# A two-layer graph network on one core: the order of the block pieces, the degree's copy and the split rows' buffers

## The chip, the core and the metric

The kernel runs on one core of a Trainium2 chip. The metric is the device time of one launch in microseconds (us); lower is better. A core has five engines that work side by side: TensorE (PE in the profile) for matmuls, VectorE (DVE) and ScalarE (ACT) for elementwise work, GpSimd (POOL), which here only issues the gathers, and SyncE (SP), which issues most of the other transfers. Each engine takes its instructions in one order that is fixed when the kernel is built, and waits at an instruction until what it depends on is there.

## The reference

There are 12,500 nodes with 256 features, and 200,000 edges sorted by their target. Both layers take the mean over each node's incoming edges:

```python
def _sage_conv(x, src, dst, W_l, b_l, W_r):
    msgs = x[src]
    agg = segment_sum(msgs, dst, num_segments=N_NODES)
    deg = segment_sum(ones, dst, num_segments=N_NODES)
    mean = agg / maximum(deg, 1.0)[:, None]
    return mean @ W_l + b_l + x @ W_r

h = relu(_sage_conv(x, src, dst, W1_l, b1, W1_r))
h = relu(_sage_conv(h, src, dst, W2_l, b2, W2_r))
out = layernorm(x + h @ W3 + b3)
```

Targets with low numbers have many edges, those with high numbers few: a target is about 12,500 times the square of a uniform number.

## The kernel before

**Two ways to sum.** Nodes lie in 98 blocks of 128. For the first targets (5 groups of 256 in layer 1, 7 in layer 2) the kernel counts the edges between every source and target into a table and multiplies it with the source rows: `count` (L622) builds the table, `product` (L604) multiplies it with rows that were split into three bf16 parts, and `degrees` (L698) sums it. `split_rows` (L598) makes the parts of x, one block at a time, with `exact` (L590): ScalarE casts, VectorE subtracts, ScalarE casts, VectorE subtracts. All this is called dense work. The other edges are gathered: `gathered` (L526) takes 4 x 128 edges in a round, fetches their source rows with four indirect transfers (L532) and sums edges with the same target by matmuls (L543). `summed` (L552) adds the result into a ring of eight blocks, `sums` and `degs`, at a place that is read from the data.

**A block's pieces.** When all edges of a block are summed, the block is finished in pieces, written as a generator. `first_block` (L852) has three in layer 1. The first loads 128 rows of x. The second turns the block's degree row into a column by a tiny matmul (L860); VectorE takes the maximum with 1 (L862) and the reciprocal (L863), and `transposed` (L812) turns the x rows with two matmuls by the identity (L814) and a ScalarE copy (L816). The third runs `sage` (L833), two matmuls by each weight, VectorE's L842 and L843, and the relu (L845), clears the ring's place, and stores h and its three parts. `last_block` (L876) has five: load h and x rows; turn the h rows; `sage`; turn the result; multiply by W3 and normalise. Blocks of the dense groups run through the same code without the degree and the clearing.

**What sets the order.** `layer` (L483) writes out the order of the TensorE and GpSimd instructions by hand. In each of its rounds (269 in layer 1, 247 in layer 2) it issues the gathers and their matmuls, then some pieces of blocks, half of the dense work that is due, the sum of the round before, more pieces, and the other half. At most `MOST` = 3 blocks are in work. A round advances a quarter of all pieces that are left, rounded up, half of them before the sum and half after; a call takes the blocks in turn from the oldest, one piece each. `begin` starts a waiting block by its first piece. Dense work is metered by costs, so that it ends eight rounds before the last. The orders of VectorE, ScalarE and SyncE come from a scheduler.

**Buffers.** Rows of x have three buffers named `x_sb`, which the split rows and the blocks share (L804). `rest` in `exact` has one buffer, which they share too, `parts` has two, and the PSUM tile `block_ps` two.

Of the kernel before, what the change touches and what calls it, by code (L numbers as in the profile page):

```python
# [7 lines left out]
F32 = mybir.dt.float32  # L8
# [5 lines left out]
OP = mybir.AluOpType  # L14
# [7 lines left out]
P = 128  # L22
# [25 lines left out]
def by_runs(  # L48
# [429 lines left out]

    AHEAD = 2

    MOST = 3

    def layer(table, hot, block, n_pieces, dense, dense_cost):  # L483


        queue, waiting, done = [], [], set()

        def advance(i):
            b, p, left = queue[i]
            next(p)  # L490
            queue[i] = b, p, left - 1
            if left == 1:
                done.add(b)
                del queue[i]
                return True

        def begin():
            while waiting and len(queue) < MOST:
                b, *of = waiting.pop(0)
                queue.append((b, block(b, *of), n_pieces))  # L500
                advance(len(queue) - 1)

        def pieces(n):

            i = 0
            for _ in range(min(n, len(queue))):
                if not advance(i):
                    i += 1
            begin()

        filler = dense(waiting)
# [58 lines left out]
        for i in range(len(rounds) + 1):  # L570

            last, before = gathered(i) if i < len(rounds) else None, last
            n = -(-sum(left for _, _, left in queue) // 4)
            pieces(-(-n // 2))
            due = dense_cost * min(1.0, (i + 1) / (len(rounds) - 8))
            fill(spent + (due - spent) * 0.5)
            if before:
                summed(*before)
                while begun < left_after(before[0]):
                    waiting.append((begun,))  # L580
                    begun += 1
                begin()
            pieces(n // 2)
            fill(due)
        fill(1e8)
        while queue or waiting:
            pieces(MOST)


    def exact(t, s):  # L590

        rest = work.tile([P, D], F32, name="rest", bufs=1)
        nc.scalar.copy(s[:, 0], t)
        nc.vector.tensor_tensor(rest, t, s[:, 0], op=OP.subtract)
# [217 lines left out]
    def transposed(t, ps, name):  # L812
        for c in range(NC):
            nc.tensor.transpose(ps[:, c], t[:, c * P:(c + 1) * P], ident)  # L814
        s = work.tile([P, NC, P], F32, name=name)
        nc.scalar.copy(s, ps[:, :NC])  # L816
        return s

    def ring(b):

# [12 lines left out]
    def sage(own_t, b, agg, wl, wr, bias, name):  # L833

        ps = block_pool.tile([P, 2, D], F32, name="block_ps")
        for c in range(NC):
            nc.tensor.matmul(ps[:, 0], lhsT=agg[:, c], rhs=wl[:, c], start=c == 0, stop=c == NC - 1)  # L837
# [7 lines left out]
        nc.scalar.activation(h, own, AF.Relu)  # L845
        return h

    def turned():
        t = block_pool.tile([P, 2, D], F32, name="block_ps")
# [2 lines left out]
    def first_block(b, agg=None):  # L852
        x_sb = load_rows(x, N, b, "x_sb")
        of_ring = agg is None
        yield True
        ps = turned()
        if of_ring:
            overlap(b, True)
            agg, deg_row = ring(b)
            nc.tensor.matmul(ps[:, NC, 0:1], lhsT=deg_row, rhs=ones[0:1, 0:1], start=True, stop=True)  # L860
            deg = work.tile([P, 1], F32, name="deg")
            nc.vector.tensor_scalar(deg, ps[:, NC, 0:1], 1.0, None, op0=OP.max)  # L862
# [12 lines left out]

    def last_block(b, agg=None):  # L876
        h_sb = load_rows(h_d, NB * P, b, "h_sb")
        x_sb = load_rows(x, N, b, "x_sb")
        of_ring = agg is None
        yield True  # L880
        if of_ring:
            overlap(b, False)
            agg, _ = ring(b)
        h_t = transposed(h_sb, turned(), "own_t")
        yield True
        h2 = sage(h_t, b, agg, w2l_sb, w2r_sb, biases[:, 1], "h")
        if of_ring:
            nc.scalar.copy(agg, zeros)
        nc.vector.tensor_add(x_sb, x_sb, biases[:, 2])
        yield True  # L890
        h2_t = transposed(h2, turned(), "own_t")
        yield True
        y = block_pool.tile([P, 2, D], F32, name="block_ps")
        for c in range(NC):
            nc.tensor.matmul(y[:, 0], lhsT=h2_t[:, c], rhs=w3_sb[:, c], start=c == 0, stop=c == NC - 1)  # L895
# [12 lines left out]
        nc.sync.dma_start(out[b * P:b * P + n, :], z[:n])  # L908
        yield True
# [383 lines left out]
```

## Time and profile before

| | |
|---|---|
| median of 3 runs | 2927.65 us (2920.19 to 2936.41) |
| the profiled execution's own time | 3466.66 us |
| its span, first to last instruction | 3464.9 us |
| mean granted TensorE clock | 0.868 |
| gathers (L532), layer 1 | 1076 x 1007 ns, from 27.2 to 1850 us |
| gathers (L532), layer 2 | 988 x 956 ns, from 1888.6 to 3405 us |
| dense product (L614) | 7056 matmuls, 289 ns |
| count casts (L688) | 1052 x 681 ns |
| turning x, h and the result (L814) | 196 x 348, 196 x 305 and 196 x 314 ns |
| own_t copy (L816) | 294 x 374 ns |
| HBM traffic | 582.80 MB read, 89.87 MB written |

The profile is of one execution, which took longer than the median of the runs without a profiler. In the views an operand pair `out<-in` tells what an instruction writes and reads, `x2` how many records a row merges (an fp32 matmul leaves two), and `[1.07 <-PE block_ps L860]` that its engine stood idle for 1.07 us until that instruction released it. A wait's three numbers are the sum in us, how often, and the longest.

### The profile page before, as it was taken

What the parts mean: (1) busy time and instruction counts of PE and PEld (TensorE: products, weight loads), DVE (VectorE), ACT (ScalarE), POOL (GpSimd) and SP (SyncE); (2) the same over time, 40 slices, a digit from 0 to 9 for tenths busy, and PEclk for the clock granted to TensorE, in tenths of its full rate; (3) what the DMA queues carried; (4) which work ended last, traced back from release to release, by engine and by line L of the source; (5) the groups of instructions that cost most, each with busy time, mean ns of one, the idle gap of its engine ahead of it and who ended that gap; (6) DMA issues with size and microseconds to landing.
All of it is one profiled execution on the core that took longest, in us unless ns stands there. A gap on an engine that the chain in (4) does not pass through costs nothing.

```text
span 3464.9 us, 54167 instructions
## 1 busy us (share of the span) xinstructions
PE 2583.9 (75%) x18630; PEld 1705.5 (49%) x18630; DVE 1468.1 (42%) x4350; ACT 1250.0 (36%) x2702; POOL 2029.7 (59%) x2074
## 2 busy tenths in 40 slices
PE   2544658778878878888886677777878887878885
PEld 1121225545545556656654354444555555656664
DVE  7656655444444444445453023333223233333433
ACT  1323655455554555556553013333111111111222
POOL 3554656665665565666663666666666666566661
PEclk9666679879979989989998888888889899999998
DMA  4544577648648648656753565666777787766762
GB/s 89 153 147 147 183 210 229 195 128 279 202 144 269 202 144 263 207 159 194 222 162 111 184 204 184 187 186 192 243 240 246 243 258 240 230 211 215 223 213 69
DMA packets 408134, 676.45 MB, mean 195 GB/s; under 512 B 59659, under 2 KB 266537, under 8 KB 407849
## 3 DMA queue, kind: packets, MB, share of 16 engines
q1 hardware_dynamic: 303415, 400.51, 36.8%
q0 software_dynamic: 99072, 270.66, 25.8%
q10 hardware_dynamic: 5362, 1.72, 0.3%
q8 instruction: 149, 2.44, 0.3%
q14 instruction: 136, 1.11, 0.1%
HBM read 582.80 MB, written 89.87 MB: 194 GB/s over the span
## 4 chain that ended last, share of the span: by engine, by line
PE 60%; issue 8%; another core or an unknown queue 8%; DVE 4%; DMA 3%; ACT 3%; SPq 0%; POOL 0%; ACTq 0%; DVEq 0%
PE dense_ps L614 22%; PE part_ps L543 8%; PE block_ps L837 6%; PE count_ps L682 6%; PE block_ps L839 5%; PE sum_ps L555 4%; PE block_ps L814 3%; PE block_ps L895 3%; ACT counts L688 1%; PE sum_ps L560 1%; DMA rows<-x_d 1%; DMA rows<-h_d 1%; PE count_ps L686 1%; DVE pick L637 1%
## 5 line engine op out<-in xcount | busy, mean ns | idle before, releaser
L532 POOL DMA_INDIRECT got<-in_x_dram,src_t x1076 | 1083.2, 1007 | 764.9 <-PE part_ps L543 282.7
L532 POOL DMA_INDIRECT got<-h_d,src_t x988 | 944.4, 956 | 610.1 <-issue 247.9
L614 PE MATMUL dense_ps<-counts,rows 128*128 128x256 bf16 x7056 | 1025.9, 289 | 84.3 <-issue 49.3
L688 ACT CAST counts<-count_ps 128x392 f32 (+2 forms) x1052 | 716.1, 681 | 633.2 <-PE count_ps L686 145.9
L614 PEld LDWEIGHTS <-rows 128*128 128x128 bf16 x7056 | 702.3, 103 | 338.0 <-issue 142.4
L543 PE MATMUL part_ps<-got,one 128*32 128x257 f32 (+1 forms) x4128 | 384.9, 438 | 96.2 <-issue 47.1
L682 PE MATMUL count_ps<-pick,low 128*128 128x392 bf16 (+2 forms) x1052 | 371.1, 381 | 104.8 <-DVE pick L637 33.3
L637 DVE TENSOR_SCALAR pick<-steps,key_t 128x686 bf16<-128x686 f16 (+2 forms) x748 | 300.0, 411 | 254.1 <-PE count_ps L682 77.3
L466 DVE TENSOR_TENSOR one<-lo_t,lane_b 128x128 f32<-128x128 bf16 x516 | 148.0, 287 | 539.6 <-PE part_ps L543 143.6
L549 ACT COPY some<-part_ps 128x257 f32<-128x257 f32 (+1 forms) x361 | 136.8, 379 | 562.0 <-remote 215.5
L567 DVE TENSOR_TENSOR sums<-sums,sum_ps 128x256 f32 x361 | 148.3, 411 | 303.2 <-remote 119.7
L555 PE MATMUL sum_ps<-two,some 128*128 128x128 f32 x1444 | 246.6, 297 | 5.4 <-remote 2.8
L555 PEld LDWEIGHTS sum_ps<-two,some 128*128 128x128 f32 x1444 | 212.6, 208 | 23.5 <-issue 8.5
L543 PEld LDWEIGHTS part_ps<-got,one 128*32 128x32 f32 x4128 | 89.9, 114 | 245.9 <-issue 178.0
L814 PE MATMUL block_ps<-ident,x_sb 128*128 128x128 f32 x196 | 50.7, 348 | 207.2 <-DVE deg L862 96.7
L842 DVE TENSOR_TENSOR own<-block_ps,biases 128x256 f32<-128x256 f32 x196 | 83.0, 423 | 259.8 <-PE block_ps L839 123.2
L682 PEld LDWEIGHTS <-low 128*128 128x128 bf16 x1052 | 108.3, 106 | 155.7 <-issue 72.1
L816 ACT COPY own_t<-block_ps 128x256 f32<-128x256 f32 x294 | 109.1, 374 | 188.7 <-PE block_ps L814 76.0
L563 DVE TENSOR_TENSOR degs<-degs,sum_ps 1x128 f32 x186 | 51.0, 274 | 232.0 <-PE part_ps L543 67.7
L895 PE MATMUL block_ps<-w_sb,own_t 128*128 128x256 f32 x392 | 122.1, 440 | 36.4 <-ACT own_t L816 25.3
L837 PE MATMUL block_ps<-w2l_sb,sums 128*128 128x256 f32 x336 | 112.6, 464 | 46.3 <-DVE sums L567 18.8
L641 DVE TENSOR_TENSOR low<-low_t,lane_b 128x512 bf16<-128x512 bf16 x187 | 128.1, 685 | 43.1 <-PE count_ps L686 28.1
(177 smaller groups left out, 2672.1 us busy)
## 6 DMA issues: line engine op xcount, KB each, us to landing
rows<-h_d SPq DMA_DIRECT2D x343, 384.0 KB
rows<-x_d SPq DMA_DIRECT2D x245, 384.0 KB
x_sb<-in_x_dram SPq DMA_DIRECT2D x291, 128.0 KB
count_d<-counts SPq DMA_DIRECT2D x28, 896.0 KB
counts<-count_d SPq DMA_DIRECT2D x28, 896.0 KB
x_d<-parts SPq DMA_DIRECT2D x98, 192.0 KB
h_d<-parts SPq DMA_DIRECT2D x98, 192.0 KB
got<-in_x_dram,src_t POOLq DMA_INDIRECT x1076
```

The lines of the kernel that those rows point to most:

```text
L532: nc.gpsimd.indirect_dma_start(out=g[:, j, :D], out_offset=None, in_=table, in_offset=bass.IndirectOffsetOnAxis(ap=src_t[:, e:e + 1], axis=0))
L543: nc.tensor.matmul(part_ps[j * W:(j + 1) * W, :width], lhsT=one[:, j], rhs=g[:, j, :width], start=r == 0, stop=r == n - 1)
L555: nc.tensor.matmul(sum_ps[:, c], lhsT=some[:, c * P:(c + 1) * P], rhs=two, start=True, stop=True)
L567: nc.vector.tensor_add(own, own, sum_ps[:, :NC])
L614: nc.tensor.matmul(ps[:, c], lhsT=rows[:, b % 2, k, c * P:(c + 1) * P], rhs=c_sb[:, b, :DN], start=False, stop=b == NB - 1 and k == 2 and ...
L637: nc.vector.tensor_scalar(r[:, :w * NB], steps[:, :w * NB], key_t[g][:, t - lo_g:t - lo_g + 1], None, op0=OP.is_equal)
L682: nc.tensor.matmul(ps[:, :(b - a) * NB], lhsT=s, rhs=r[:, a * NB:b * NB], start=True, stop=alone)
L688: nc.scalar.copy(to[:, :, bass.ds(n0 + a, b - a)], ps[:, :(b - a) * NB].rearrange("p (d s) -> p s d", s=NB))
L814: nc.tensor.transpose(ps[:, c], t[:, c * P:(c + 1) * P], ident)
L837: nc.tensor.matmul(ps[:, 0], lhsT=agg[:, c], rhs=wl[:, c], start=c == 0, stop=c == NC - 1)
L839: nc.tensor.matmul(ps[:, 1], lhsT=own_t[:, c], rhs=wr[:, c], start=c == 0, stop=c == NC - 1)
L895: nc.tensor.matmul(y[:, 0], lhsT=h2_t[:, c], rhs=w3_sb[:, c], start=c == 0, stop=c == NC - 1)
```

## The change

Three things change. A round has three places instead of two; each advances at most one piece of one block, the oldest that is allowed, and two pieces of a block lie at least `APART` = 2 places apart. At most two blocks are in work, and one is begun at a time. The sum of the round before stands in the last of the three places, and the dense work that is due is dealt out in thirds. Second, the degree column is copied out of PSUM by the same ScalarE copy as the turned rows (257 columns instead of 256), and VectorE works on the copy in SBUF. Third, split rows are loaded into two buffers of their own (`split_sb`), `x_sb` has two instead of three, and `exact` writes its remainder over the tile that it is given instead of into `rest`. In `last_block` the load of x moves behind the third piece's work, and the addition of the bias behind the turning of the result.

```diff
-    MOST = 3
+    MOST, APART = 2, 2
...
         def begin():
-            while waiting and len(queue) < MOST:
+            if waiting and len(queue) < MOST:
                 b, *of = waiting.pop(0)
-                queue.append((b, block(b, *of), n_pieces))
-                advance(len(queue) - 1)
-
-        def pieces(n):
-
-            i = 0
-            for _ in range(min(n, len(queue))):
-                if not advance(i):
-                    i += 1
+                p = block(b, *of)
+                next(p)
+                queue.append([b, p, n_pieces - 1, turn + APART])
+
+        def pieces():
+            nonlocal turn
+            turn += 1
+            q = next((q for q in queue if q[3] <= turn), None)
+            if q:
+                next(q[1])
+                q[2:] = q[2] - 1, turn + APART
+                if q[2] == 0:
+                    done.add(q[0])
+                    queue.remove(q)
             begin()
...
-            n = -(-sum(left for _, _, left in queue) // 4)
-            pieces(-(-n // 2))
             due = dense_cost * min(1.0, (i + 1) / (len(rounds) - 8))
-            fill(spent + (due - spent) * 0.5)
-            if before:
-                summed(*before)
-                while begun < left_after(before[0]):
-                    waiting.append((begun,))
-                    begun += 1
-                begin()
-            pieces(n // 2)
-            fill(due)
+            for part in range(3):
+                if part == 2 and before:
+                    summed(*before)
+                    while begun < left_after(before[0]):
+                        waiting.append((begun,))
+                        begun += 1
+                pieces()
+                fill(spent + (due - spent) / (3 - part))
...
-    def exact(t, s):
-
-        rest = work.tile([P, D], F32, name="rest", bufs=1)
+    def exact(t, s, rest):
+
         nc.scalar.copy(s[:, 0], t)
...
     def split_rows(b):
-        t = load_rows(x, N, b, "x_sb")
+        t = load_rows(x, N, b, "split_sb")
         s = work.tile([P, 3, D], BF16, name="parts")
-        exact(t, s)
+        exact(t, s, t)
...
     def load_rows(table, n_rows, b, name):
-        t = work.tile([P, D], F32, name=name, bufs=MOST if table is x else 2)
+        t = work.tile([P, D], F32, name=name)
...
-        s = work.tile([P, NC, P], F32, name=name)
-        nc.scalar.copy(s, ps[:, :NC])
-        return s
+        s = work.tile([P, NC * P + 1], F32, name=name)
+        n = NC * P + more
+        nc.scalar.copy(s[:, :n], ps.rearrange("p c l -> p (c l)")[:, :n])
+        return s[:, :NC * P].rearrange("p (c l) -> p c l", l=P), s[:, NC * P:]
...
-            deg = work.tile([P, 1], F32, name="deg")
-            nc.vector.tensor_scalar(deg, ps[:, NC, 0:1], 1.0, None, op0=OP.max)
+        x_t, deg = transposed(x_sb, ps, "own_t", int(of_ring))
+        if of_ring:
+            nc.vector.tensor_scalar(deg, deg, 1.0, None, op0=OP.max)
             nc.vector.reciprocal(rdeg[:, b:b + 1], deg)
-        x_t = transposed(x_sb, ps, "own_t")
         yield True
-        h = sage(x_t, b, agg, w1l_sb, w1r_sb, biases[:, 0], "h")
+        h, own = sage(x_t, b, agg, w1l_sb, w1r_sb, biases[:, 0], "h")
...
-        exact(h, s)
+        exact(h, s, own)
...
     def last_block(b, agg=None):
         h_sb = load_rows(h_d, NB * P, b, "h_sb")
-        x_sb = load_rows(x, N, b, "x_sb")
...
             nc.scalar.copy(agg, zeros)
+        x_sb = load_rows(x, N, b, "x_sb")
+        yield True
+        h2_t, _ = transposed(h2, turned(), "own_t")
         nc.vector.tensor_add(x_sb, x_sb, biases[:, 2])
-        yield True
-        h2_t = transposed(h2, turned(), "own_t")
         yield True
```

More of the change, by code (lines that the diff above doesn't have):

```diff
@@ L479, in by_runs @@
     AHEAD = 2
-    MOST = 3
+    MOST, APART = 2, 2
     def layer(table, hot, block, n_pieces, dense, dense_cost):
         queue, waiting, done = [], [], set()
[L488 to L495, printed above, removed]
+        turn = 0
         def begin():
-            while waiting and len(queue) < MOST:
+            if waiting and len(queue) < MOST:
                 b, *of = waiting.pop(0)
-                queue.append((b, block(b, *of), n_pieces))
-                advance(len(queue) - 1)
-        def pieces(n):
-            i = 0
-            for _ in range(min(n, len(queue))):
-                if not advance(i):
-                    i += 1
+                p = block(b, *of)
[11 more added lines that the diff above has]
+                    queue.remove(q)
             begin()
@@ L572, in layer @@
             last, before = gathered(i) if i < len(rounds) else None, last
[L573 to L574 removed]
             due = dense_cost * min(1.0, (i + 1) / (len(rounds) - 8))
[L576 to L584 removed]
+            for part in range(3):
[6 more added lines that the diff above has]
+                fill(spent + (due - spent) / (3 - part))
         fill(1e8)
         while queue or waiting:
[L587 to L592 removed]
+            pieces()
+    def exact(t, s, rest):
         nc.scalar.copy(s[:, 0], t)
@@ L810, in load_rows, with transposed @@
         return t
-    def transposed(t, ps, name):
+    def transposed(t, ps, name, more=0):
         for c in range(NC):
             nc.tensor.transpose(ps[:, c], t[:, c * P:(c + 1) * P], ident)
-        s = work.tile([P, NC, P], F32, name=name)
-        nc.scalar.copy(s, ps[:, :NC])
-        return s
+        s = work.tile([P, NC * P + 1], F32, name=name)
+        n = NC * P + more
+        nc.scalar.copy(s[:, :n], ps.rearrange("p c l -> p (c l)")[:, :n])
+        return s[:, :NC * P].rearrange("p (c l) -> p c l", l=P), s[:, NC * P:]
     def ring(b):
@@ L845, in sage @@
         nc.scalar.activation(h, own, AF.Relu)
-        return h
+        return h, own
     def turned():
@@ L883, in last_block @@
             agg, _ = ring(b)
-        h_t = transposed(h_sb, turned(), "own_t")
+        h_t, _ = transposed(h_sb, turned(), "own_t")
         yield True
-        h2 = sage(h_t, b, agg, w2l_sb, w2r_sb, biases[:, 1], "h")
+        h2, _ = sage(h_t, b, agg, w2l_sb, w2r_sb, biases[:, 1], "h")
         if of_ring:
             nc.scalar.copy(agg, zeros)
+        x_sb = load_rows(x, N, b, "x_sb")
+        yield True
+        h2_t, _ = transposed(h2, turned(), "own_t")
         nc.vector.tensor_add(x_sb, x_sb, biases[:, 2])
-        yield True
-        h2_t = transposed(h2, turned(), "own_t")
         yield True
```

## The prediction

> **What bounds the kernel now.** I read the page first, then TensorE's waits, the stages, the timeline around one degree step, and GpSimd's groups. From the page:
>
> ```profile
> span 3464.9 us, 54167 instructions
> ...
> PE 2583.9 (75%) x18630; PEld 1705.5 (49%) x18630; DVE 1468.1 (42%) x4350; ACT 1250.0 (36%) x2702; POOL 2029.7 (59%) x2074
> ...
> PE 60%; issue 8%; another core or an unknown queue 8%; DVE 4%; DMA 3%; ACT 3%; SPq 0%; POOL 0%; ACTq 0%; DVEq 0%
> ```
>
> TensorE is busiest and holds 60% of the chain that ended last. It works in a fixed program order, so a matmul that waits holds everything behind it. It is idle for 3464.9 - 2583.9 = 881 us. What ends these gaps, from TensorE's waits (us in total, times, longest):
>
> ```profile
> PE block_ps L814 <- DVE deg L862: 96.7, 70, 3.9
> PE block_ps L814 <- DMA x_sb<-in_x_dram: 78.0, 7, 15.2
> PE block_ps L814 <- ACT h L845: 58.9, 31, 5.5
> ...
> PE block_ps L860 <- DVE degs L563: 31.6, 19, 7.9
> PE block_ps L837 <- DVE sums L567: 31.6, 18, 5.8
> ...
> PE block_ps L895 <- ACT own_t L816: 25.3, 17, 4.6
> ...
> PE block_ps L814 <- DVE rest L594: 19.4, 2, 17.9
> ```
>
> Nearly all of the listed waits stand in a block's pieces, the code that the change touches. The first kind in the timeline:
>
> ```profile
> 1019.04 0.55 PE L860 MATMUL block_ps<-ones,degs 1*128 1x1 f32 x2
> ...
> 1020.87 0.16 DVE L862 TENSOR_SCALAR deg<-block_ps 128x1 f32<-128x1 f32 x1 [1.07 <-PE block_ps L860]
> ...
> 1021.08 0.44 PE L814 MATMUL block_ps<-ident,x_sb 128*128 128x128 f32 x2 [1.49 <-DVE deg L862]
> ```
>
> TensorE turns the degree row, stands 1.49 us until VectorE has read it, and only then turns the rows of x into the same PSUM tile. By stage (set-up left out):
>
> ```profile
> 27.00:510.00 483.00, 237.45 (x1219) 101.97 (x1219) 329.64 (x945) 192.59 (x393) 268.01 (x256) 0.72 0.51 153
> 510.00:1890.00 1380.00, 1129.99 (x8831) 758.02 (x8831) 636.61 (x1893) 731.42 (x1503) 816.21 (x822) 0.89 0.63 196
> 1890.00:3465.00 1575.00, 1214.52 (x8572) 843.93 (x8572) 492.31 (x1480) 325.97 (x806) 943.32 (x987) 0.89 0.67 208
> ```
>
> Columns: length, then busy time of TensorE, its weight loads, VectorE, ScalarE, GpSimd; granted clock, DMA share, GB/s. After 510 us TensorE is busy about 80%, nobody else above 60%. The second limit is GpSimd, whose gathers run at 0.949 us each (median) with 0.30 us between: 4 x 1.25 = 5.0 us a round, against (1849.9 - 510) / 205 = 6.5 us in the first layer after the splits and (3404.4 - 1888.6) / 247 = 6.1 us in the second.
>
> **The change part by part.** Sums are against the profiled execution (3466.66 us: the span and 1.8 us around it), in us of TensorE standing still.
>
> Degree copied with the turned rows. The transposes no longer wait for VectorE; ScalarE's copy takes 257 columns for 256. Removed: 96.7. Added on ScalarE: L549 has both widths, 384 ns at 257 and 373 at 256, so 88 x 0.011 = 1. VectorE runs the same two small operations (153 and 157 ns, the first from PSUM, the second from SBUF), but the first now waits for ScalarE. In the timeline the degree matmul ends at 1019.6; with the transposes (0.44), ScalarE's wait at the own_t copy (76.0/95 = 0.8) and the copy (0.37) VectorE is released at 1021.2, 0.3 later than now, with one more hand-over 0.6 at most. Queued behind it are the picks, the "one" selections and the additions to sums, for which TensorE waits. Bound: 0, if the picks made two ahead cover it, to 88 x 0.6 = 53. I take 18, a third, since VectorE is 46% busy there. It could also gain: VectorE's own wait at L862 is 39 now.
> A rule speaks against: the Trainium skill, GPSIMD Engine Reference, Key points, says that GpSimd shares its SBUF interfaces with VectorE and contends with instructions in a two-port mode. The operation moves from PSUM to SBUF, 88 x 0.15 = 13 us of it. By the rule GpSimd might lose all 13. By the rows, a gather takes 1007 ns on average in layer 1, with 966 us of VectorE work beside it, and 956 in layer 2: 1076 x 0.051 = 55, or 0.06 us for each us, so 1. I take the row: nothing.
>
> Split rows in buffers of their own. In the first stage a block's x rows share three buffers with the 98 split rows: at 159.8 us TensorE stands 15.06 us for one such load. Seven waits on the load and two on "rest" make 78.0 + 19.4 = 97. In the built order of SyncE's queue the loads for blocks now stand one to two blocks ahead, waiting only for TensorE. I take 85 removed; the bound is 0, if a load still sits behind split loads, to 97. The splits themselves get two buffers for three, but no shared "rest": 98 in some 440 us, 4.5 us each, against a chain of four 0.4 us operations and a load, so nothing; uncovered, a late split would hold the first dense product, some 7 us (one wait of 6.9 stands there now).
> The page TensorE: Matmul & The Clock Gate, HAM oscillation, says that gaps above some 3.4 us bring the clock to half. The row agrees in kind: 0.72 in this stage, 0.89 after. By the rule the seven gaps cost 7 x 1.7 = 12 more, an estimate (half of 3.4 each); by the row, 237 x (1 - 0.72/0.89) = 45 of busy time, most of it not for these gaps. TensorE stays half idle in this stage, so the middle gets 0; the 45 belong to the good rival.
>
> Pieces one at a time, two places apart. Three places in a round for two. A block's pieces now lie at least 2/3 of a round apart, and half a round before: 1/6 of 6.1 = 1.0 us more. The 31 waits for h (1.9 each) lose 31, bound 0 to 59; the 17 + 2 for own_t (25.3 + 6.9) lose 19, bound 0 to 32. The degree matmul stood right behind the gather matmuls in 85 of 88 blocks, now in 4 of 88: a third of a 6.5 us round later, 2.2 us, against waits of 1.8 for degs (31.6 + 11.6 at the ring's end): 35 of 43. A product straight behind its sum stood in 18 places, now 9; but the usual distance from sum to product falls from half a round to a third. Of 31.6 I take 5, bound -30 to +16.
> In layer 2 the x load moves behind the second piece and its addition behind the transposes. On SyncE it passes "rows" and result stores, but in the built order it stays over 20 us of TensorE work (by the row durations) ahead of its use; SyncE's holds before "rows" loads come out alike in both orders, under the cover of three "rows" buffers. Nothing; without that cover the last blocks pay one landing, about 3. Two blocks in flight are enough: three places a round serve 0.75 blocks of four pieces, and blocks come at 0.5 at most. The tail behind the last gather has 21 groups of matmuls for 20: nothing.
>
> Sum: 97 + 85 + 31 + 19 + 35 + 5 - 18 = 254 of 881. Not all comes off the end: a stall removed often becomes the next wait, for a pick, a count cast or a landing gather. TensorE's waits on VectorE, ScalarE and DMA sum to 331 + 185 + 126 = 642, while the chain holds only 10% of the span on these, 346: a share of 0.54. So 254 x 0.54 = 137: 3467 becomes 3330.
>
> To the median. The profiled execution is 539 us longer than 2927.65. Scaled alike, the gain is 137 x 0.845 = 116, giving 2812. If the busy times hold and only idle shrinks (2928 - 2584 = 344 of 881), it is 53, giving 2874. The gathers' constant 943 to 949 ns speak for the second, waits made of round trips for the first. I take the middle: 2840.
>
> **The rivals.** (1) All of it counts: each stall is on the path and the clock rises. 254 x 0.845 = 215: 2713. For: TensorE is the only engine near full after 510 us. Against: the chain's 10%. (2) Gathers bind without a profiler: 2064 x 1.25 = 2578, plus 27 before the first, 38 between layers, 61 behind the last, is 2704 at the least, and part of the remaining 224 would be their landings. Then the stalls are hidden: 2925. Against: GpSimd waits 371 us for L543, so TensorE leads. (3) Slower: VectorE is held at the degree operation. Place: layer 1's 88 ring blocks. If the copy stands behind four count casts (2.39 us at 1011.99), the hold is 2 x 0.35 + 2.39 + 0.37 = 3.5, and TensorE starves for picks: 88 x 3.5 - 254 = 54 lost, about 2970. It decides from 254/88 = 2.9 a block. Against: the 0.8 us at which the copy waits for TensorE now, so ScalarE is mostly ahead.
>
> **How the numbers follow.** A measurement tells some 0.5% from no change. The forecast, 2790 to 2890: 0.50. Rival 1, 2700 to 2790: 0.18. Between forecast and no change: 0.06. Rival 2: 0.12. Rival 3: 0.14. Faster 0.74, same 0.12, slower 0.14. The range 2725 to 2950 leaves out a tenth at each end.
>
> **What would show it.** TensorE's wait on the degree and on the x load gone, that on h and degs halved, idle below 700 us; VectorE's wait at the degree under 1 us a block; the first stage shorter than 483 us. Wrong if GpSimd's gap stays at 0.30 us almost throughout, or if picks appear high among TensorE's waits.

## The result and the profile after

The changed kernel takes 2916.39 us (median of 11 runs, 2906.07 to 2920.58), the kernel before 2933.88 us on the same chip (11 runs). The ratio is 0.9938, with a 95% interval of 0.9917 to 0.9958: 17 us or 0.6% faster. The prediction said 2840 us, 88 us or 3% faster. The profiled execution of the changed kernel has a span of 2904.3 us and a time of its own of 2906.07 us. From its page:

```profile
span 2904.3 us, 54103 instructions
...
PE 2393.2 (82%) x18630; PEld 1631.3 (56%) x18630; DVE 1476.0 (51%) x4350; ACT 1251.7 (43%) x2702; POOL 2037.4 (70%) x2074
...
PE 52%; DMA 20%; POOL 10%; issue 7%; DVE 6%; ACT 4%; SPq 0%; DVEq 0%; ACTq 0%; POOLq 0%
```

TensorE is busy for 82% of the span where the first profile showed 75%, and the chain no longer holds "another core or an unknown queue", which had 8% before. These are not doings of the change: the later runs showed that the first profile, 3466.66 us, came from another kind of chip than the median of 2927.65 us. On one kind the kernel before takes about 2930 to 2940 us, on the other about 3430 to 3460 us, with a profile and without one. Each of the five chips of the later runs was measured within one stretch of time, so "kind" names what was measured there and not a lasting property of a chip. All that is compared below is compared on one chip or on chips of one kind, or is said to be across kinds; "the quicker kind" is that of the metric.

TensorE's waits in the changed kernel (sum in us, how often, longest):

```profile
PE part_ps L543 <- DMA got<-h_d,src_t: 122.0, 56, 14.0
PE block_ps L858 <- DVE own L841: 49.4, 5, 19.3
...
PE block_ps L811 <- ACT h L843: 31.6, 30, 2.4
```

The waits on the degree and on the load of x are gone, as predicted. The wait on h is there, at 31.6 us in 30 places, and in the second place stands one that the kernel before has not: the degree matmul, now L858, waits for VectorE's L841 on `own`. The stages (columns as before: length, busy time of TensorE, its weight loads, VectorE, ScalarE and GpSimd, granted clock, DMA share, GB/s):

```profile
27.00:510.00 483.00, 282.05 (x1560) 134.97 (x1561) 353.03 (x1013) 214.15 (x434) 305.96 (x288) 0.77 0.60 182
510.00:1890.00 1380.00, 1229.16 (x10229) 844.71 (x10228) 706.51 (x2078) 782.50 (x1618) 1007.99 (x1023) 0.95 0.74 234
1890.00:2904.00 1014.00, 879.35 (x6836) 649.80 (x6833) 406.01 (x1228) 254.25 (x651) 720.43 (x754) 0.95 0.81 258
```

In the middle stage TensorE is busy 1229 of 1380 us and GpSimd has sent off 1023 gathers, one in 1.35 us. A degree step of the changed kernel, with what comes ahead of it, in the timeline:

```profile
361.65 0.42 ACT L843 ACTIVATE h<-own 128x256 f32<-128x256 f32 x1 [0.89 <-DVE own L841]
...
392.62 0.41 ACT L589 CAST parts<-split_sb 128x256 bf16<-128x256 f32 x1 [3.61 <-DMA split_sb<-in_x_dram]
...
393.25 0.41 ACT L589 CAST parts<-h 128x256 bf16<-128x256 f32 x1 [0.22 <-DMA x_d<-parts]
...
394.58 0.48 DVE L592 TENSOR_TENSOR parts<-own,parts 128x256 bf16<-128x256 f32 x1
...
395.10 0.42 DVE L840 TENSOR_TENSOR own<-block_ps,biases 128x256 f32<-128x256 f32 x1
...
396.79 0.41 ACT L589 CAST parts<-split_sb 128x256 bf16<-128x256 f32 x1 [2.23 <-DMA x_d<-parts]
...
397.22 0.42 DVE L590 TENSOR_TENSOR split_sb<-split_sb,parts 128x256 f32<-128x256 f32 x1 [1.70 <-ACT parts L589]
397.56 0.48 DVE L841 SCALAR_TENSOR_TENSOR own<-block_ps,rdeg,own 128x256 f32<-128x256 f32 x1
...
398.10 0.58 PE L858 MATMUL block_ps<-ones,degs 1*128 1x1 f32 x2 [11.37 <-DVE own L841]
...
398.61 0.69 PE L811 MATMUL block_ps<-ident,x_sb 128*128 128x128 f32 x2
...
399.60 0.36 ACT L814 COPY own_t<-block_ps 128x257 f32<-128x257 f32 x1
...
399.99 0.15 DVE L861 TENSOR_SCALAR own_t<-own_t 128x1 f32<-128x1 f32 x1 [0.34 <-ACT own_t L814]
```

The last four lines are the degree's path as it was meant to be: the transposes (L811) follow the degree matmul without a wait, ScalarE copies 257 columns, and VectorE takes the degree from SBUF. The lines above them are the new wait. The degree matmul stands for 11.37 us because its PSUM tile is freed by L841. L840 has to wait for `own`, which the block before still has as the remainder of `exact`; it starts when L592, the last to use it, ends at 395.06. That block had its h at 361.65 (L843), but the first cast of its `exact` (L589 from h) came only at 393.25. In between ScalarE made this cast for nine split rows, and stood 3.61 us before the last one for that row's load; the block's own cast then waited 0.22 us for a store of parts, `x_d<-parts`, to free a buffer. L841 in turn stands in VectorE's order behind the subtraction of one more split row, which another store of parts held (2.23 us at its cast). So the block's remainder waits in the queue of the split rows, for their loads and for their stores.

### The profile page after: what moved, and what is told of

Its sections match the earlier page's. It is cut to its first block, busy times and chain, and to the rows that moved or that the text cites. A ratio compares the mean times of both kernels' runs of the same rounds, so it can differ in the third digit from the quotient of the medians.

```text
span 2904.3 us, 54103 instructions
## 1 busy us (share of the span) xinstructions
PE 2393.2 (82%) x18630; PEld 1631.3 (56%) x18630; DVE 1476.0 (51%) x4350; ACT 1251.7 (43%) x2702; POOL 2037.4 (70%) x2074
## 4 chain that ended last, share of the span: by engine, by line
PE 52%; DMA 20%; POOL 10%; issue 7%; DVE 6%; ACT 4%; SPq 0%; DVEq 0%; ACTq 0%; POOLq 0%
PE dense_ps L610 18%; POOL got L532 10%; PE part_ps L543 7%; DMA got<-h_d,src_t 6%; PE block_ps L835 6%; PE count_ps L678 5%; PE block_ps L837 4%; PE sum_ps L555 4%; DMA rows<-h_d 3%; DMA x_sb<-in_x_dram 3%; DMA got<-in_x_dram,src_t 3%; DMA rows<-x_d 3%; PE block_ps L811 2%; PE block_ps L893 2%; DMA split_sb<-in_x_dram 2%
## 5 line engine op out<-in xcount | busy, mean ns | idle before, releaser
L532 POOL DMA_INDIRECT got<-in_x_dram,src_t x1076 | 1091.0, 1014 | 468.7 <-issue 270.0
L610 PE MATMUL dense_ps<-counts,rows 128*128 128x256 bf16 x7056 | 980.3, 280 | 51.7 <-DMA rows<-x_d 26.3
L610 PEld LDWEIGHTS <-rows 128*128 128x128 bf16 x7056 | 672.3, 100 | 287.1 <-issue 86.8
L543 PE MATMUL part_ps<-got,one 128*32 128x257 f32 (+1 forms) x4128 | 356.3, 418 | 199.1 <-DMA got<-h_d,src_t 122.0
L678 PE MATMUL count_ps<-pick,low 128*128 128x392 bf16 (+2 forms) x1052 | 347.2, 356 | 49.9 <-DVE pick L633 30.3
L543 PEld LDWEIGHTS part_ps<-got,one 128*32 128x32 f32 x4128 | 85.9, 111 | 326.6 <-issue 163.7
L555 PE MATMUL sum_ps<-two,some 128*128 128x128 f32 x1444 | 234.9, 287 | 0.2 <-DVE sums L567 0.2
L840 DVE TENSOR_TENSOR own<-block_ps,biases 128x256 f32<-128x256 f32 x196 | 82.9, 423 | 242.1 <-PE block_ps L837 241.2
L814 ACT COPY own_t<-block_ps 128x256 f32<-128x256 f32 (+1 forms) x294 | 110.0, 375 | 121.2 <-PE block_ps L811 118.9
L843 ACT ACTIVATE h<-own 128x256 f32<-128x256 f32 x196 | 81.4, 415 | 179.6 <-DVE own L841 179.6
L682 PE MATMUL count_ps<-aft,low 128*128 128x98 bf16 x614 | 132.8, 216 | 0.0
L835 PE MATMUL block_ps<-w1l_sb,sums 128*128 128x256 f32 x352 | 117.3, 463 | 6.6 <-ACT own_t L814 4.1
L837 PE MATMUL block_ps<-w1r_sb,own_t 128*128 128x256 f32 x392 | 112.6, 414 | 0.0
```

Of the source, the lines that this page charges most:

```text
L532: nc.gpsimd.indirect_dma_start(out=g[:, j, :D], out_offset=None, in_=table, in_offset=bass.IndirectOffsetOnAxis(ap=src_t[:, e:e + 1], axis=0))
L543: nc.tensor.matmul(part_ps[j * W:(j + 1) * W, :width], lhsT=one[:, j], rhs=g[:, j, :width], start=r == 0, stop=r == n - 1)
L555: nc.tensor.matmul(sum_ps[:, c], lhsT=some[:, c * P:(c + 1) * P], rhs=two, start=True, stop=True)
L610: nc.tensor.matmul(ps[:, c], lhsT=rows[:, b % 2, k, c * P:(c + 1) * P], rhs=c_sb[:, b, :DN], start=False, stop=b == NB - 1 and k == 2 and ...
L678: nc.tensor.matmul(ps[:, :(b - a) * NB], lhsT=s, rhs=r[:, a * NB:b * NB], start=True, stop=alone)
```

## Theories

**P, stalls replaced.** A stall of TensorE costs time where TensorE is what is late; the change gains little because its removed stalls are smaller on the metric's chip than the first profile said, and because a new one, on `own`, takes the place of the load's. **G, gathers bind.** GpSimd issues gathers back to back, and TensorE's stalls are hidden behind them (the prediction's second rival). They are told apart by leaving out half of the gathers, by doing each part alone, and by giving `own` or the parts buffers of their own.

## The parts on the slower kind of chip

These five kernels ran on chips of the slower kind, e1 to e4 on one and e5 on another. e1 is the kernel before. e2 is the degree's copy alone:

```diff
-            nc.vector.tensor_scalar(deg, ps[:, NC, 0:1], 1.0, None, op0=OP.max)
-        x_t = transposed(x_sb, ps, "own_t")
+        x_t, deg = transposed(x_sb, ps, "own_t", int(of_ring))
+            nc.vector.tensor_scalar(deg, deg, 1.0, None, op0=OP.max)
```

e3 is the new order alone (`MOST, APART`, three places in a round, nothing of `last_block`'s moved load, `x_sb` with its three buffers), e4 both of them, and e5 the changed kernel as it is.

> The kernel before once more, unchanged, for a second profile. Theory G (the gathers bind: GpSimd issues one each 1.25 us, 5.0 us a round, and TensorE's stalls lie under that; the first profile of before was stretched by waits that the plain runs do not have): span near 2930 us, layer 2 at 5.0 to 5.2 us a round, GpSimd's gap at 0.30 us, TensorE's waits on gathers over 100 us. Theory P (TensorE binds, and the gain was given back by new waits in the changed kernel): layer 2 at 5.5 us a round or more, hardly any wait of TensorE on gathers.

> Before, with only the degree column copied with the turned rows. Theory G: the stall on the degree goes, but only layer 1 can use it: 0 to 10 us faster. Theory P: 40 to 80 us faster, since the stall is on TensorE's path.

> Before, with only the order of the pieces changed (three places, two blocks, two places apart; x_sb keeps three buffers shared with the split rows). Theory G: within 10 us of before. Theory P: the new waits come with the order: 20 to 60 us slower than before.

> Before, with the order and the degree copy, without the split rows' buffers and the later load of x in layer 2. Theory G: -10 to 0 us against before; what is missing to the changed kernel (-17 us) is the work of the split buffers in the first stage. Theory P: slower than before by 0 to 40 us, the split buffers bring the rest.

> The changed kernel again, beside the kernel before. The runs so far fall on two sorts of chip, one on which before takes 2930 us and one on which it takes 3430. Theory G (the gathers bind where TensorE keeps up): if this chip is of the 2930 sort, -10 to -30 us as measured; if of the 3430 sort, where gathers do not run back to back, more than order and degree together, -50 to -140 us. Theory P (stalls given back by new waits): a ratio near 0.994 on either.

| kernel | us | to the kernel before on the same chip |
|---|---|---|
| e1 before | 3428.8 | (3428.97, 18 runs) |
| e2 degree | 3395.56 | 0.992 (0.989 to 0.995) |
| e3 order | 3404.18 | 0.9929 (0.9902 to 0.9956) |
| e4 order and degree | 3383.85 | 0.9893 (0.9858 to 0.9928) |
| e5 the whole change | 3399.3 | 0.992 (0.989 to 0.9951) |

e1 shows that 3430 us is this chip's time for the kernel, not the profiler's doing: its 18 runs without the change have the same median as the one with a profile. The degree brings 0.8% and the order 0.7%, where the prediction's sums by 0.54 gave them 79 x 0.54 / 3467 = 1.2% and 90 x 0.54 / 3467 = 1.4%; together they bring about 1.1%. The whole change is not better than these two: what it has beside them, the buffers of the split rows and the later load of x in `last_block`, shows no gain (e13 below has the buffers alone; the later load was not run alone). Neither theory's figures for e2, e3 and e4 came: they gained 33, 25 and 45 us, where G allowed 10 at most, and P had 40 to 80 for e2 and no gain for e3 and e4. For e5 P's ratio near 0.994 came, and G's 50 us or more did not. e2 also prices the conversion: 99.4 us of waits on the degree on such a chip (e9 below) gave 0.8% of 3429, 27 us (17 to 38): between a sixth and two fifths.

## Half of the gathers left out

Two of the four groups of a round are fetched, the others keep a constant, so part of the sum is left out. All matmuls, casts and stores stay.

```diff
-            for j in range(G):
+            for j in range(2):
                 e = t0 + j * n + r - C0 * P
                 nc.gpsimd.indirect_dma_start(
```

> Before with half of the gathers: only two of the four groups of 128 edges in a round are fetched, the matmuls and everything else stay; the other half of the edge rows is a constant, so that part of the sum is left out. GpSimd then needs 2.5 us a round for 5.0. Theory G: on a 2930 chip 150 to 350 us faster, since the next limit (TensorE with its stalls) takes over. Theory P: at most 60 us faster, as TensorE binds anyway.

> The changed kernel with the same half of the gathers left out. Theory G: the stalls that the change removes now count: 100 to 250 us faster than before with half of the gathers. Theory P: within 40 us of it.

> The kernel before with half of the gathers left out (two of the four groups of a round; the others stay at a constant, so part of the sum is left out), as the anchor for the two below. Both theories: 2700 us within 12.

> The changed kernel with half of the gathers left out, again, beside the one above on the same chip. Both theories expect 2669 us within 15, whatever the sort of chip: without the load of the gathers the chips don't differ.

The kernel before takes 2700.32 us (e6) and 2702.24 us (e14), the changed one 2668.57 (e7) and 2662.74 us (e12). The four came from three chips of the slower kind, where the whole kernel takes 3425 to 3461 us: with half of the gathers the granted clock is 0.95 for 0.87, and the unknown queue's 8% of the chain are gone. TensorE binds here: it is busy for 86% of e14's span, and GpSimd waits 1056 us for L543's matmuls in e6. So this is where a stall of TensorE ought to show in full. That e6 is 727 us below the whole kernel on its chip (3427.55 us) is far more than P's 60: on the slower kind the gathers, or what comes with them, cost the whole kernel more than TensorE's work can explain. The whole change is worth 32 us (e6 to e7), within P's 40 and not G's 100 to 250, where the prediction took off 137. Then one part and two parts in this regime:

> The degree copied with the turned rows, alone, with half of the gathers left out. By the prediction's price (96.7 us of waits, 0.54 of them on the path) about 43 us less than the anchor after the 18 given back. By the price of this regime (the waits on the degree measured 25 us in 75 places, 0.33 us each) 10 to 25 us less.

> The new order and the degree's copy, without the split rows' buffers, with half of the gathers left out. If the split rows' buffers gain nothing (theory P), this is within 10 us of the changed kernel with half of the gathers, 2663 to 2669. By the prediction's step it is 40 us or more above it, since the x load's waits, 69 us in this regime, stay.

TensorE's waits in the anchor (e14):

```profile
PE block_ps L814 <- DMA x_sb<-in_x_dram: 55.7, 8, 13.3
...
PE block_ps L814 <- DVE deg L862: 24.9, 76, 1.6
PE block_ps L814 <- ACT h L845: 24.4, 33, 3.4
```

The degree's copy alone takes 2675.69 us: 26.5 less than the anchor, against 24.9 us of waits in e14's row. Where TensorE binds, this wait counts one for one, and what VectorE's later hold gives back (18 us in the prediction) doesn't show. Order and degree take 2661.14 us: the order brings 14.6 more, though the waits on h stay (24.4 us in e14, 25.6 in e16). The changed kernel, which has the split rows' buffers in addition, is no better (2662.74 in e12, on another chip): e16 still has 61.2 us of waits on the load, e12 has none and 41.6 us on `own` in their place.

## Where the split rows' gain went

e13 is the kernel before with the third part alone: `split_sb`, and the remainder over the given tile. Layer 2's result rows `z` take the buffers of `split_sb`, which stand idle there; so it is in e10, e11 and e17.

```diff
-        t = load_rows(x, N, b, "x_sb")
+        t = load_rows(x, N, b, "split_sb")
-        exact(t, s)
+        exact(t, s, t)
...
-        exact(h, s)
+        exact(h, s, own)
```

> The kernel before with the split rows in two buffers of their own and the remainder written over the given tile, nothing else (x_sb keeps its three buffers, its order stays; the result rows z take the split rows' buffers in layer 2 so that it fits). By the prediction's step: the x load's and the remainder's waits, 78 and 19 us, go, and 85 x 0.54 = 46 us with them, ratio about 0.987. By theory P (a remainder in own is held by the block before, and the stall comes back at the next block's tile): the x load's waits go, waits for own of about 30 to 50 us stand in their place, ratio 0.995 to 1.003.

3459.13 us in 22 runs against 3460.64 in 27: the ratio is 1.0002 (0.9987 to 1.0017). TensorE's waits:

```profile
PE block_ps L813 <- DVE deg L861: 111.4, 74, 5.1
...
PE block_ps L859 <- DVE own L842: 45.2, 4, 19.9
```

The rows for the load of x and for "rest", 78.0 + 19.4 us in the first profile, are gone, and `own` stands there with 45.2 us in four places (waits on `split_sb` add 18 us in ten places, but 10 of these are on the result rows `z`, which have that name in layer 2). As theory P had it, nothing is gained. Two edits of the changed kernel ask what holds `own`. e10 (whole) and e11 (half of the gathers) give it two buffers; e17 (half) leaves it one, and gives the blocks a buffer for their parts which the split rows don't use:

```diff
-        own = work.tile([P, D], F32, name="own", bufs=1)
+        own = work.tile([P, D], F32, name="own")
```

```diff
-        s = work.tile([P, 3, D], BF16, name="parts")
+        s = work.tile([P, 3, D], BF16, name="h_parts", bufs=1)
         exact(h, s, own)
```

> The changed kernel with two buffers for own (the result rows z take the place of the split rows' buffers in layer 2, where these stand idle, so that it fits). Theory P: the waits of the degree matmul for own (L858, 49 us in five places) come from own being held as the remainder of the block before, so they go, and about 15 to 40 us with them (1%). Theory G: the waits go too, but the time stays within 10 us of the changed kernel, since the gathers run on meanwhile. If the waits stay, own's single buffer isn't their cause.

> The same with half of the gathers left out (two of the four groups of a round; the others stay at a constant, so part of the sum is left out). TensorE binds here, so that a wait removed shows in full: both theories expect 25 to 45 us less than the changed kernel with half of the gathers if own's single buffer holds the degree matmul; no difference if it doesn't.

> The changed kernel with half of the gathers left out (part of the sum is left out), in which the blocks' three parts have a buffer of their own (h_parts, one) instead of the two that they share with the split rows. own keeps its single buffer. If own is held because a block's remainder waits for a buffer of parts behind the split rows, the waits of L858 for own (42 us in five places) fall to under 15 and the time by 15 to 30 us against 2663 to 2669. If VectorE's order or own's single buffer is what holds it, they stay above 25 and the time within 10 us.

With two buffers for `own`, e11 takes 2653.68 us (2645.97 to 2656.5), 9 less than e12 on the same chip (2660.19 to 2680.9; four runs each); L858's wait falls only from 41.6 us (5) to 31.5 (3). So `own`'s single buffer is a small part of it there, and the 25 to 45 us expected of e11 didn't come. With parts of their own, e17 takes 2628.97 us, 34 less than e12. This is a comparison across chips: e17 ran on one of the quicker kind, and no other half kernel did, so a part of the 34 may be the chip's. The rows are clearer. The largest waits for `own` in e17:

```profile
who waited for it (us, times):
  ACT h L843: 164.8, 96
  PEld block_ps L811: 35.7, 43
  PE block_ps L811: 23.7, 30
  DVE h_parts L592: 22.6, 42
  ACT h_parts L591: 8.1, 19
...
```

L858, with 41.6 us the first of e12's rows, has no wait for `own` any more, and TensorE is idle 314 us (2632.1 - 2318.1) for 352 (2659.9 - 2308.0), though one new wait of 11.2 us came, of a count's matmul on VectorE's degree operation. The kind of chip doesn't explain that the wait is gone, since the changed kernel has it on the quicker kind too (49.4 us).

The time from a block's relu (L843 in the changed kernel) to the first cast of its `exact`, for the blocks whose h came before 480 us, says the same:

| kernel | us from h to the first cast |
|---|---|
| before (e1 and e18, one of each kind) | 0.4 to 14 |
| the third part alone (e13) | 16 to 44 |
| the whole change (its profile; e12) | 21 to 50; 20 to 33 |
| blocks with their own parts (e17) | 0.4 to 3.5 |

What held `own` was the queue for the two `parts` buffers: the change gave the split rows their own load buffers, but left them and the blocks one pair of `parts`, and with the remainder in `own` it tied the block's PSUM tile to that pair. The whole kernel e10, with two buffers for `own`, takes 3370.17 us against 3425.02, ratio 0.9839 (0.9798 to 0.9881), where the changed kernel has 0.992 (0.989 to 0.9951) on a chip of the same kind. It is ahead of both kernels there, 29 us below e5, where P expected 15 to 40. But L858's wait for `own` falls by 12 us only (27.6 us in two places in e5, 15.5 in one in e10). Its gain is larger than that and than e11's 9 us, and why is not shown. The whole kernel with `h_parts` wasn't run.

e8 asked whether slower split rows would help: the changed kernel with their cost at 1.4.

```diff
-    COST_DENSE, COST_DEGREES, COST_SPLIT = 0.7, 1.6, 0.8
+    COST_DENSE, COST_DEGREES, COST_SPLIT = 0.7, 1.6, 1.4
```

> The changed kernel with the split's cost in the plan raised from 0.8 to 1.4, so that the first stage's dense work is spread over more rounds. Theory G: the first stage is where gathers do not run back to back (288 of a possible 386 in 483 us), so a thinner first stage gives 15 to 60 us against the changed kernel. Theory P: TensorE's work is only moved: 0, or up to 40 us slower.

3389.47 us, ratio 0.9883 (0.9849 to 0.9917), 10 us under e5 on the same chip, with overlapping intervals: not decided. The waits of L858 for `own` are there (40.6 us in four places), so spacing alone doesn't remove them.

## The kernel before on the quicker kind of chip

e9 and e18 are the kernel before again, for a profile on the metric's kind of chip. e9 fell on the slower kind (3433.5 us), e18 on the quicker one.

> The kernel before, unchanged, for its profile. If this chip is of the quicker sort, both theories expect about 2930 us. Theory G (the gathers bind there): 1.25 to 1.27 us from gather to gather in layer 2, about 5.1 us a round, GpSimd's idle 0.3 us almost throughout, and the degree waits at about 0.4 us each for 1.4. Theory P (the stalls held the end): GpSimd stands behind TensorE as in the first profile, with a round above 5.3 us. If it is of the slower sort: about 3430 us and the profile of the first one, which tells nothing new.

> The kernel before, unchanged, for its profile, in case the chip is of the quicker sort. Theory G there: about 2930 us, gathers 1.25 to 1.27 us apart in layer 2, the degree waits near 0.35 us each, no share of another core or an unknown queue in the chain. Theory P: about 2930 us with rounds above 5.3 us and GpSimd behind TensorE. On the slower sort: 3430 us, and about 8% of the chain without a cause in the program, as in the first profile.

2927.77 us, beside a median of 2942.02 in 7 runs on this chip. Its page and TensorE's waits:

```profile
span 2926.0 us, 54167 instructions
...
PE 2385.2 (82%) x18630; PEld 1631.3 (56%) x18630; DVE 1476.2 (50%) x4350; ACT 1256.9 (43%) x2702; POOL 2034.0 (70%) x2074
...
PE 51%; DMA 17%; POOL 7%; issue 5%; DVE 4%; ACT 2%; DVEq 0%; SPq 0%; ACTq 0%; POOLq 0%
```

```profile
PE part_ps L543 <- DMA got<-h_d,src_t: 112.8, 49, 11.1
PE block_ps L814 <- DMA x_sb<-in_x_dram: 85.2, 9, 18.3
...
PE block_ps L814 <- ACT h L845: 30.2, 31, 3.0
...
PE block_ps L837 <- DVE sums L567: 25.2, 21, 3.5
...
PE block_ps L814 <- DVE deg L862: 22.3, 79, 1.2
...
PE block_ps L860 <- DVE degs L830: 3.1, 5, 1.0
...
PE block_ps L895 <- ACT own_t L816: 1.5, 3, 0.5
```

This is the profile that the prediction should have been worked from. The load of x, a wait for a transfer, is as large as in the first one (85.2 for 78.0). The waits that are hand-overs between engines are a fraction: the degree 22.3 us for 96.7 (0.28 us each for 1.38), degs 3.1 for 31.6, own_t 1.5 for 25.3, h 30.2 for 58.9. TensorE's largest wait is for landing gathers. Of its 541 us of idle time (2926.0 - 2385.2) the changed kernel has 511 (2904.3 - 2393.2): 30 less, of which 8 went into longer busy time. That is the difference of the spans, 21.7 us. These are one execution of each kernel, on two chips of the quicker kind whose medians for the kernel before differ by 8 us, so the rows show where the time went and not every microsecond of it.

Where these 22 us arise is seen by counting gathers in equal windows, the kernel before and then the changed one (the count behind GpSimd's time is the number of gathers and little else; one gather is 1.25 us):

```profile
27.00:270.00 243.00, 117.25 (x606) 49.16 (x605) 187.68 (x556) 70.92 (x131) 143.65 (x134) 0.79 0.50 148
270.00:520.00 250.00, 171.54 (x1136) 92.24 (x1135) 180.85 (x506) 161.54 (x335) 174.31 (x167) 0.79 0.76 231
520.00:1560.00 1040.00, 956.93 (x8198) 660.94 (x8197) 582.31 (x1720) 680.43 (x1391) 764.93 (x772) 0.96 0.76 237
1600.00:2840.00 1240.00, 1059.14 (x8250) 770.22 (x8251) 461.02 (x1367) 306.98 (x744) 916.59 (x960) 0.95 0.82 258
```

```profile
27.00:270.00 243.00, 134.59 (x672) 58.24 (x673) 199.67 (x567) 66.88 (x121) 158.41 (x146) 0.80 0.47 141
270.00:520.00 250.00, 156.85 (x958) 82.89 (x957) 158.38 (x461) 153.14 (x325) 152.31 (x148) 0.75 0.72 222
520.00:1560.00 1040.00, 972.33 (x8324) 668.92 (x8324) 596.18 (x1757) 684.70 (x1412) 777.47 (x781) 0.96 0.76 241
1600.00:2840.00 1240.00, 1071.65 (x8412) 779.71 (x8413) 470.89 (x1411) 318.75 (x768) 933.32 (x977) 0.95 0.82 262
```

To 270 us the changed kernel is 12 GpSimd instructions ahead: TensorE doesn't stand 46.5 us for the load of x there. From 270 to 520 us it loses 19, because the five waits on `own` all lie there, 49.4 us against 38.7 for the load, and GpSimd stands 49.7 us behind L543 for 25.1. From 520 to 1560 us it wins 9 back, 11 us, where 20 of the degree's 22 us of waits lay. In all layer 1 is 3 us shorter (first to last gather 1535.4 for 1538.1 us). In layer 2 it wins 17, 21 us. These are the whole gain, and most of them come after 2500 us. TensorE's waits from 2500 to 2800 us, before and then changed:

```profile
PE block_ps L837 <- DVE sums L567: 16.6, 13, 2.5
PE block_ps L814 <- ACT h L845: 5.8, 10, 1.8
```

```profile
PE block_ps L811 <- ACT h L843: 11.0, 11, 2.1
PE block_ps L835 <- DVE sums L567: 1.6, 2, 0.9
```

A product's wait for its sum falls from 16.6 to 1.6 us; the wait on h even grows. TensorE is busy for 286 of these 300 us instead of 273, GpSimd waits 6 us for L543 instead of 12 and 2 us for the turning of rows (L814, now L811) instead of 13, and 11 more gathers go out. That the new order is what shortened the wait for the sums fits these rows, but no part of the change was run alone on this kind of chip.

So neither theory holds alone. In layer 2 a round takes 1253.3 / 247 = 5.07 us, 1274.9 / 247 = 5.16 before, against 4 x 1.255 = 5.02 of gathers back to back: G is nearly right there, and only some 35 us were to be had, of which 22 came. In layer 1 gathers back to back would take 1411 us (1076 x 1.311). With half of the gathers, where TensorE binds, layer 1 took 1477 us (e14's first to last gather, on the slower kind), and the whole kernel takes 1538. This speaks for stalls that count there, and P says what became of them.

## Why the prediction was wrong, step by step

**What bounds the kernel: the wrong chip's profile.** "Scaled alike" or "if the busy times hold" treated the 539 us between the profiled execution and the median as something that a factor removes. They were another chip's stalls, and the waits priced were partly these. The line "another core or an unknown queue 8%", 277 us of a program that uses one core, was in the first fence and has no place in the prediction's sums. Every slower chip's profile of a whole kernel that was read has such a share, of 6 to 10%; neither e18 nor the changed kernel's does.

**Degree: the term 96.7 - 18 = 79.** Its mechanism was right: the wait is gone everywhere. Its size on the metric's chip is 22.3 us. VectorE does stand at the operation, 31.4 us in 36 places in the changed kernel, but the half kernels show no loss from it: 26.5 us gained for 24.9 waited. The third rival, VectorE held, didn't come about. For the contention on the way from PSUM to SBUF the row was the better guide: gathers of layer 1 take 1014 ns in the mean for 1011, 1076 x 0.003 = 3 us at most and not the 13 that the rule of shared interfaces (the Trainium skill, GPSIMD Engine Reference, Key points) would have made.

**Split rows: "I take 85 removed".** This step failed outright. The load's waits went, and 49.4 us on `own` came in the same stage; the part alone has a ratio of 1.0002 (0.9987 to 1.0017). The bound was set at a load that might still sit behind split loads. Not considered was that `exact` also takes a buffer of `parts`, that the edit put the block's `own` into it, and that `own` holds a PSUM tile that the next block's first matmul needs. The good rival's 45 us of clock did not come either. The row has nothing: the first stage's granted clock is 0.78 in e18 and 0.77 in the changed kernel. The rule on gaps (the Trainium skill, TensorE: Matmul & The Clock Gate, HAM oscillation) agrees once all gaps are counted: TensorE has 12 above 3.4 us in this stage in e18 and 13 in the changed kernel, so by the rule no clock was to be won. Nor did the first stage get shorter, as the prediction's signs had it: by 510 us GpSimd has done 288 instructions for 293.

**Order: 31 + 19 + 35 + 5 = 90.** h was to lose half; it lost nothing (30.2 to 31.6 us, and 24.4 to 25.6 in the half kernels). own_t and degs had 1.5 and 3.1 us to lose on this chip. Sums, taken at 5 "of a bound of -30 to +16", fell from 25.2 to 12.4, and are the row that fits layer 2's gain. The order alone is worth 0.7% (e3) and 14.6 us where TensorE binds: right in sign. Which row brings it there is open: with half of the gathers the wait on sums falls by 4 us only (18.3 in e15, 14.2 in e16), and on the slower kind it scatters too much to tell (31.6, 82.0 and 69.1 us in three profiles of the kernel before).

**The share of 0.54.** One factor for all stages was wrong both ways: near 1 for the degree where TensorE binds, 0.17 to 0.38 for it on the slower chip, and 0 for the split rows. With e18's waits and the prediction's own steps the sum would have been 22 + 75 + 15 + 1 + 3 + 5 - 18 = 103, and by 0.54, with nothing to scale, 2872; without the split rows, which failed by their own step, 28 and 0.54 give 15, and 2913. The run gave 2916. So two steps carry the error: the hand-over waits taken at the slower chip's length, and the 85 us of the split rows.

**The rivals.** The first, 2713 us, needed all stalls on the path. The second, 2925 us, is the nearest to the result, and right on layer 2; it was given 0.12 because the slower chip's rounds of 6.1 us hid how near the gathers are to back to back.

## What stays open, and what was not expected of the hardware

What the slower kind of chip does differently isn't settled. A gather's median is much the same (941 to 949 ns on the slower kind, 946 on the quicker), but TensorE's granted clock is 0.87 for 0.92, and engines stand still together. Work on another core of the same chip, which the name "another core" in the chain would fit, is not ruled out. An example from the changed kernel on the slower kind (e5):

```profile
2307.84 0.37 ACT L549 COPY some<-part_ps 128x256 f32<-128x256 f32 x1 [2.08 <-remote]
2307.84 0.29 DVE L466 TENSOR_TENSOR one<-lo_t,lane_b 128x128 f32<-128x128 bf16 x1 [4.98 <-remote]
...
2308.07 0.94 POOL L532 DMA_INDIRECT got<-h_d,src_t  x1 [1.59 <-remote]
...
2308.26 1.01 PE L543 MATMUL part_ps<-got,one 128*32 128x256 f32 x8 [2.05 <-issue]
```

ScalarE, VectorE and GpSimd go on within 0.23 us of each other, by a releaser that the profile can't name ("remote"), and TensorE follows after 2.05 us without a cause shown. It goes with the gathers: with half of them left out both kernels ran on such chips with a clock of 0.95, and the degree's wait was 0.33 us each (24.9 / 76 in e14). Whether it is the number of gathers, their bytes or their row sizes wasn't tried.

## What to carry to other kernels

Before a wait is priced, the profiled execution's own time is held against the median: if they differ by a sixth, as here, and the chain names a cause that the program hasn't got, the profile doesn't stand for the runs of the median, and hand-over waits in it are not to be taken at their length. When two users of a buffer are parted, follow every other buffer that the same helper takes, and above all what the new owner of a scratch tile keeps busy: here a remainder moved into `own` handed the next block's PSUM tile to the split rows' queue. And a removed stall is counted by stage, by what that stage's slowest engine got done in the same window, not by one share for the whole kernel.
